# A two-layer graph network on one core: the late constants get due times of their own, and the one-hots are laid out block by block

## The chip, the core and the metric

The kernel runs on one core of a Trainium2 chip. A core has a matrix engine (TensorE, PE in the profile, with its weight loads as PEld), a vector engine (VectorE, DVE), an engine for copies and activation functions (ScalarE, ACT), a general engine (GpSimd, POOL) and a queue engine for transfers (SyncE, SP). Each runs its own list of instructions in order; semaphores join the lists. The metric is the time of one execution on the device in microseconds; several executions are run and their median is taken.

## The reference

Both layers work on 128 graphs of 128 nodes with 64 features, and a weighted adjacency matrix `adj` for each graph, of which about 6% of the entries are set.

```python
def _L0_gnn_ref(x, adj, W1, b1, W2, b2):
    mask = (adj > 0.0).astype(x.dtype)
    W1a, W1b = (W1[:F], W1[F:])
    xj_proj = x @ W1a
    diff = x[:, :, None, :] - x[:, None, :, :]
    h = jax.nn.relu(xj_proj[:, :, None, :] + diff @ W1b + b1)
    hm = jnp.einsum('bjkh,bjk->bjh', h, mask)
    deg = jnp.sum(mask, axis=-1)
    return hm @ W2 + deg[..., None] * b2
def _L1_gnn_ref(feat, adj, W1, b1, W2, b2, W3, b3):
    agg = jnp.einsum('bmn,bnd->bmd', adj, feat)
    h = jax.nn.elu(agg @ W1 + b1)
    h = jax.nn.elu(h @ W2 + b2)
    out = h @ W3 + b3
    return out
x = _layernorm(x + _L0_gnn_ref(...))
x = _layernorm(x + _L1_gnn_ref(...))
```

The costly part is layer 0: for each edge (j, k) a vector of 192 values, its relu, and the sum over the edges of each node j.

## The kernel before

**Pairs, blocks and units.** Two graphs make a pair; there are 64 pairs. The nodes of a graph are sorted by degree (`prepare`, `sort_x`, `sort_mask`), so that the sorted nodes fall into nine fixed blocks: nodes p0 to p1 of block i get s edge slots each, which makes n = s (p1 - p0) columns, between 66 and 170, and E = 1323 columns over all blocks. One block of one pair is a unit. A unit has three steps (`unit`): ScalarE copies the node's own part `aj` into one of four PSUM banks `e` (L910), TensorE adds the neighbours' part `cp` by 18 matmuls of a block's one-hot `oh` (L920, in three bf16 parts, three thirds of the 192 values, two graphs), and VectorE sums the absolute values over the slots into `sums` (L930). Bank u mod 4 is free for unit u + 4 when unit u is reduced. The one-hots say which neighbour each slot of each node takes; VectorE makes one block of both graphs by one comparison of the running count `vp` with the slot number `slotc` (L675).

**Around the units.** Each pair goes through `prepare` (mask `mk` L545, keys, ranks `cmp` L568, permutation `permb` L575), `sort_x` (sorted features, projection L606, `aj` L613, correction `ea` L635 with matmuls L626 and L629, `sa` L620, `corr` L642 on GpSimd), `sort_mask` (matmuls L246 and L248, `mtp`, `permT`, `vp` L668, then the nine one-hots), `turn` and `project_c` (`cp` through matmuls L708 and L711, casts L718, the rest `r` L722 on VectorE, L725, L727 on GpSimd). `finish` does the remainder: `hm` (L842), the projection L847 and L851, back to the old order L864, the norm (`y` L737, `st` L742), and layer 1 with L871, L880, L886, L893 and `h` (L797).

**What sets the order.** The program emits the instructions itself, in the order that `Flow` picks. Each piece of work is a thread, a generator whose steps name an engine, an estimated cost and what they come after. Every step has a due time in a model of the machine, taken from the table `DUE` and from the start of its pair, at 11.1651 units of the model per pair. Of the steps that the model says can start, `Flow.run` takes the one with the least due time; early on it first takes those that the model can start earliest. When a thread's list of due times has run out, all its later steps keep the last one. The chosen order is the order of every engine's list; on the chip only semaphores hold an instruction. These semaphores are put in from the tiles that instructions write and read.

**The late constants.** `consts_late` (L484 on) prepares what layer 1 and the second projection need: w2d (VectorE), v1p (ScalarE), a tile of ones (`onesf`), two matmuls for sums of weights (L504, L505), the biases `cc` (L508 to L510), the centred last weights (L512 to L519), and the last bias as three bf16 rows `rowp` (L521 and L362 to L366). They are 22 steps, nearly all on VectorE, each small and most waiting for the one before. The thread starts at half a pair before pair 0, with one due time for all its steps.

Of the kernel before, what the change touches and what calls it, by code (L numbers as in the profile page):

```python
# [32 lines left out]
BF16 = mybir.dt.bfloat16  # L33
# [153 lines left out]
def sparse(tc, env):  # L187

    g = type("env", (), dict(env))
    nc, P, N, F, H, O, HB, H1, NP, E = (  # L190
        g.nc, g.P, g.N, g.F, g.H, g.O, g.HB, g.H1, g.NP, g.E)
    LAY, NB = g.LAY, g.NB
    loads, prep, work, ps_m = g.loads, g.prep, g.work, g.ps_m
# [3 lines left out]
    flow = Flow([ps_m.tile([P, 512], F32, name=f"m{i}") for i in range(4)])  # L197
# [4 lines left out]
    ROUND = 11.1651  # L202
    AHEAD = 4

    DUE = {
        "prepare": (-43.06, -42.93, -39.21, -39.08, -35.87),
        "sort_x": (-26.76, -10.46, -10.33, -3.14, -3.02, 2.5, 2.63, 2.76, 2.89),
        "sort_mask": (-26.12, -25.99, -25.86, -23.42, -23.29, -23.16, -13.67, -13.28, -13.03,
                      -12.77, -2.63, -2.25, -1.99, -1.73),
        "turn": (-36.9, -36.77),  # L210
        "project_c": (-32.15, -29.32, -29.2, -29.07, -28.94, -4.17, -4.04),
        "finish": (12.64, 19.44, 19.57, 21.62, 21.75, 21.88, 22.01, 28.04, 28.17, 29.2, 33.56,
                   33.69, 33.82, 34.71, 43.31, 43.44, 44.47, 44.6, 46.52, 46.65, 48.06, 48.19,
# [2 lines left out]
                 (4.68, 4.81, 4.94), (5.07, 5.2, 5.33), (5.97, 6.1, 6.22), (6.35, 6.48, 6.61),  # L216
                 (7.25, 11.61, 11.74)],
    }

    def begin_thread(name, p, gen):  # L220
        flow.start(ROUND * p, DUE[name], gen)
# [262 lines left out]
    def consts_late():  # L484

        v = nc.vector

        def w2diag():
            for s in range(2):
                h = slice(s * HB, (s + 1) * HB)  # L490
                v.tensor_scalar(w2d[h, :, s, :], w2s[h], 0.5, None, op0=OP.mult)
        yield from op("DVE", 0.5, w2diag, "w2d", "w2", "w2d0")

        def v1diag():
            for s in range(2):
                nc.scalar.copy(v1p[s * F:(s + 1) * F, s, :], v1d[s * F:(s + 1) * F])
        yield from op("ACT", 0.6, v1diag, "v1p", "v", "v1p01")


        onesf = temp([P, P], F32, "onesf")  # L500
        yield from op("DVE", 0.2, lambda: v.memset(onesf, 1.0), "onesf")

        def sums(t):
            nc.tensor.matmul(t[:, O:O + 1], v2s, onesf[:, 0:1], start=True, stop=True)  # L504
            nc.tensor.matmul(t[:, :O], onesf, v3s, start=True, stop=True)  # L505
        ev, t = yield ("PE", 0.6, made("onesf", "v", "c"), 1, sums)
        c3 = rows[:, :O]
        ev, = yield ("DVE", 0.2, [ev], 0, lambda: v.tensor_sub(cc[:, 3:4], cc[:, 3:4], t[:, O:O + 1]))  # L508
        ev, = yield ("DVE", 0.2, [ev], 0, lambda: v.tensor_scalar(cc[:, 0:2], cc[:, 2:4], -1.0, None, op0=OP.mult))
        ev, = yield ("DVE", 0.2, [ev], 0, lambda: v.tensor_scalar(cc[:, 2:4], cc[:, 2:4], 1.0, None, op0=OP.add))  # L510
        happened(ev, "const", "cc")
        ev, = yield ("DVE", 0.2, [ev], 0, lambda: v.tensor_sub(c3, c3, t[:, :O]))  # L512
        flow.give(t, ev)

        for k, w in enumerate((v3s, c3)):
            m = mean[:, k:k + 1]
            for fn in (lambda: v.tensor_reduce(m, w, AX.X, OP.add),
                       lambda: v.tensor_scalar(m, m, 1.0 / O, None, op0=OP.mult),
                       lambda: v.tensor_scalar(w, w, m, None, op0=OP.subtract)):  # L519
                ev, = yield ("DVE", 0.2, [ev], 0, fn)  # L520
        ev, = yield ("DVE", 0.2, [ev], 0, lambda: v.tensor_copy(rows[:, O:], c3))  # L521
        happened(ev, "const", "v3s")
        happened(ev, "const", "rows")
        last = ["rows", "rowp0", "b2p"]
        for name, fn in parts(rows, rowp, NR):
            yield from op("DVE", 0.4, lambda: fn(nc.vector), "row" + name, *last)
            last = ["row" + name]
        happened(event("const", "row2"), "const", "rowp")
# [116 lines left out]
    def sort_mask(p, ev):  # L645

        d, a, permb = S[p], ADJ[p], S[p]["permb"]

        def sort(t):
            for s in range(2):  # L650
                stationary(t[:, s * N:(s + 1) * N], lambda h: d["mk"][:, s, h], permb[:, s, :],
                           start=True, stop=True)
            for s in range(2):
                stationary(t[:, (2 + s) * N:(3 + s) * N], lambda h: permb[:, s, h], identb,
                           start=True, stop=True)
        ev, t = yield ("PE:*", 0.22, [ev], 1, sort)
        mtp = d["mtp"] = prep.tile([P, 2, N], BF16, name="mtp", bufs=7)
        permT = d["permT"] = prep.tile([P, 2, N], F32, name="permT", bufs=7)
        evm, = yield ("ACT", act(2 * N), [ev], 0, lambda: nc.scalar.copy(flat(mtp), t[:, :2 * N]))
        happened(evm, "mtp", p)  # L660
        ev, = yield ("ACT", act(2 * N), [ev], 0, lambda: nc.scalar.copy(flat(permT), t[:, 2 * N:]))
        flow.give(t, ev)
        happened(ev, "permT", p)
        ev, vps = yield ("PE:*", 0.12, [evm] + made("prefix"), 1,
                         lambda vps: stationary(vps[:, :2 * N], lambda h: prefix[:, h], flat(mtp),
                                                start=True, stop=True))
        vp = prep.tile([P, 2, N], BF16, name="vp")
        ev, = yield ("ACT", act(2 * N), [ev], 0, lambda: nc.scalar.copy(flat(vp), vps[:, :2 * N]))  # L668
        flow.give(vps, ev)
        oh = d["oh"] = prep.tile([P, 2, E], BF16, name="oh", bufs=5)  # L670
        for i, (base, n, p0, p1, sl) in enumerate(LAY):
            w = p1 - p0
            c = slice(base, base + n)
            ev, = yield ("DVE PORT", 0.08 + n / 960, [ev] + made("slotc"), 0,
                         lambda: nc.vector.tensor_tensor(  # L675
                             oh[:, :, c].rearrange("p b (s w) -> p b s w", w=w),
                             vp[:, :, p0:p1].rearrange("p b (o w) -> p b o w", o=1)
                             .to_broadcast([P, 2, sl, w]),
                             slotc[:, c].rearrange("p (b s w) -> p b s w", b=1, w=w)
                             .to_broadcast([P, 2, sl, w]),  # L680
                             op=OP.is_equal))
            happened(ev, "oh", p, i)
# [219 lines left out]
    def unit(u, ev):  # L902
        p, i = units[u]
        d = S[p]
        base, n, p0, p1, sl = LAY[i]
        w = p1 - p0
        e = edges[u % NE][:, :3 * n]
        ev, = yield ("ACT", 0.09 + 3 * n / 1200,
                     [ev, event("aj", p)] + made("banks"), 0,
                     lambda: nc.scalar.copy(  # L910
                         e.rearrange("p (c s w) -> p c s w", c=3, w=w),
                         d["aj"][:, :, p0:p1].rearrange("p c (o w) -> p c o w", o=1)
                         .to_broadcast([P, 3, sl, w])))

        def gather():
            cp, oh = d["cp"], d["oh"]
            for k in range(3):
                for c in range(3):
                    for s in range(2):
                        nc.tensor.matmul(e[s * HB:(s + 1) * HB, c * n:(c + 1) * n],  # L920
                                         cp[:, k, s, c * HB:(c + 1) * HB],
                                         oh[:, s, base:base + n],
                                         start=False, stop=(k == 2), skip_group_check=True)
        flow.under_way = u < len(units) - 14
        ev, = yield ("PE:t", 0.03 + 0.0037 * n, [ev, event("cp", p), event("oh", p, i)], 0, gather)

        def reduce():
            if "sums" not in d:
                d["sums"] = work.tile([P, 3, N], F32, name="sums")
            nc.vector.tensor_reduce(d["sums"][:, :, p0:p1],  # L930
                                    e.rearrange("p (c s w) -> p c w s", c=3, w=w),
                                    AX.X, OP.add, apply_absolute_value=True)
        ev, = yield ("DVE", 0.07 + 3 * n / 960, [ev], 0, reduce)
        happened(ev, "sums", p, i)
        return ev
# [33 lines left out]
    flow.start(-97.0, [0.0], consts_wad())  # L969
    flow.start(DUE["sort_x"][2], [0.0], consts_b2())  # L970
    flow.start(-95.0, [0.0], consts_banks())
    flow.start(ROUND * -0.5, [0.0], consts_late())
    for k in range(NE):
        begin_unit(k, [0.0])
    arrive_late()
# [203 lines left out]
```

## Time and profile before

| what | value |
|---|---|
| runs | 758.67, 760.54, 761.2 us; median 760.54 us |
| the profiled execution | a span of 758.2 us from the first to the last instruction; the fastest run shown is 758.67 |
| mean granted clock of TensorE | 0.988 |
| gather matmuls L920 | 10368, 393.3 us busy |
| reduces L930 | 576, 334.4 us busy |
| copies into e, L910 | 576, 293.6 us busy |
| one-hots L675 | 576, 148.9 us busy |

The page gives each engine's busy time, slices of the span, the chain of work that ended last, and groups of instructions by line. In a line of the timeline the first number is the start, the second the length, then engine, source line, operation, what is written and read, and how many instructions were merged; in brackets stands how long the engine had been idle and who released it. A line of the waits names who waited for whom, the total, the number of times and the longest. Spans of one engine's neighbours overlap a little[...]. Windows give, for each engine, the busy time and the number of instructions in a stretch, then the granted clock of TensorE as a share of the full one, and the DMA share and rate.

### The profile page before, as it was taken

Reading aid. Unit: us, or ns where it says so; the run is one execution under the profiler, and the core shown is the slowest. Engines: PE = TensorE matmul, PEld = TensorE weight load, DVE = VectorE, ACT = ScalarE, POOL = GpSimd, SP = SyncE. Lnnn points to the kernel's source line nnn. Section 1 sums busy time; section 2 is a strip of 40 time slices with the busy share of each in tenths; the row PEclk is TensorE's granted clock in tenths of the full one; section 3 lists DMA queues with packets and bytes.
Section 4 is the critical chain, followed back from the end, with each engine's and each line's share of the span. In section 5 each row is a group of like instructions: output and inputs, shape, how many; then the busy total and the mean of one; then the engine's idle time right before and its main releaser. Section 6 shows DMA issues by size and latency. Waiting matters only on the chain.

```text
span 758.2 us, 36118 instructions
## 1 busy us (share of the span) xinstructions
PE 736.3 (97%) x14788; PEld 672.4 (89%) x14789; DVE 722.5 (95%) x2381; ACT 705.7 (93%) x1986; POOL 432.4 (57%) x801
## 2 busy tenths in 40 slices
PE   7699999999999999999999999999999999999994
PEld 4588999999999999999999999999999999999993
DVE  7799999999999999999999999999999999999984
ACT  4499999999999999999999999999999999999984
POOL 5255566566556557556556656655655655655662
PEclk9799999999999999999999999999999999999998
DMA  4000011011011011011101101101101101100000
GB/s 121 15 3 3 17 31 31 17 31 32 16 31 32 20 27 31 20 27 31 28 20 31 31 17 32 31 16 31 31 20 28 31 21 27 31 21 16 10 13 19
DMA packets 54667, 19.72 MB, mean 26 GB/s; under 512 B 37600, under 2 KB 54496, under 8 KB 54496
## 3 DMA queue, kind: packets, MB, share of 16 engines
q1 hardware_dynamic: 53792, 17.05, 9.3%
q8 instruction: 118, 1.93, 1.1%
q14 instruction: 53, 0.43, 0.2%
q10 hardware_dynamic: 704, 0.30, 0.2%
HBM read 13.14 MB, written 4.19 MB: 23 GB/s over the span
## 4 chain that ended last, share of the span: by engine, by line
PE 95%; DVE 2%; ACT 1%; DMA 1%; issue 0%; POOL 0%; POOLq 0%; SPq 0%; DVEq 0%; ACTq 0%
PE e L920 46%; PE m L606 6%; PE m L708 5%; PE m L847 5%; PE m L886 4%; PE m L880 4%; PE m L893 4%; PE m L864 3%; PE m L246 3%; PE m L690 3%; PE m L592 2%; PE m L871 2%; PE m L851 1%; PE m L711 1%; PE m L248 1%; PE m L691 1%
## 5 line engine op out<-in xcount | busy, mean ns | idle before, releaser
L920 PE MATMUL e<-oh,cp 128*64 128x162 bf16 (+3 forms) x10368 | 393.3, 229 | 6.0 <-DVE oh L675 5.6
L920 PEld LDWEIGHTS <-cp 128*64 128x64 bf16 x10368 | 357.8, 110 | 18.3 <-issue 6.6
L930 DVE TENSOR_REDUCE sums<-e 128x54 f32<-128x486 f32 (+8 forms) x576 | 334.4, 608 | 10.2 <-PE e L920 4.6
L910 ACT COPY e<-aj 128x504 f32<-128x504 f32 (+6 forms) x576 | 293.6, 543 | 3.1 <-DVE sums L930 2.6
L749 POOL TENSOR_SCALAR ve<-st 128x2 f32<-128x2 f32 x126 | 24.1, 191 | 242.4 <-DVE st L742 237.0
L675 DVE TENSOR_TENSOR oh<-vp,slotc 128x308 bf16<-128x308 bf16 (+6 forms) x576 | 148.9, 315 | 4.8 <-ACT vp L668 1.3
L750 POOL TENSOR_TENSOR rs<-ve,mhalf 128x2 f32<-128x2 f32 x126 | 87.8, 697 | 10.5
L727 POOL TENSOR_TENSOR cp<-r,cp 128x512 bf16<-128x512 f32 x64 | 74.5, 1164 | 32.0 <-ACT cp L725 32.0
L642 POOL TENSOR_TENSOR corr<-ea,sa 128x384 f32<-128x384 f32 x64 | 64.3, 1005 | 16.5 <-DVE ea L635 11.5
L791 ACT ACTIVATE r<-m,cc 128x256 f32<-128x256 f32 x128 | 61.4, 480 | 5.2 <-PE m L880 3.2
L842 POOL TENSOR_TENSOR hm<-sums,corr 128x384 f32<-128x384 f32 x63 | 63.2, 1004 | 4.0 <-DVE sums L930 4.0
L620 POOL TENSOR_TENSOR sa<-aj,srow 128x384 f32<-128x384 f32 x64 | 64.3, 1005 | 1.0 <-ACT aj L613 1.0
L613 ACT ACTIVATE aj<-m,b1c 128x128 f32<-128x128 f32 x192 | 56.5, 366 | 8.2 <-PE m L606 1.2
L797 DVE SCALAR_TENSOR_TENSOR h<-m,cc,e 128x256 f32<-128x256 f32 x128 | 60.3, 471 | 2.0 <-ACT e L794 1.9
L794 ACT ACTIVATE e<-r 128x256 f32<-128x256 f32 x128 | 54.4, 426 | 2.1
L606 PE MATMUL m<-xsT,wad 128*128 128x128 f32 x384 | 53.7, 276 | 0.0
L847 PE MATMUL m<-w2d,hm 128*128 128x128 f32 x384 | 53.5, 276 | 0.0
L722 DVE TENSOR_TENSOR r<-m,cp 128x256 f32<-128x256 f32 x128 | 47.7, 414 | 1.6 <-ACT cp L718 1.6
L771 ACT ACTIVATE x<-y,nb,rs 128x64 f32<-128x64 f32 x126 | 49.0, 441 | 0.2 <-POOL nb L753 0.2
L718 ACT CAST cp<-m 128x256 bf16<-128x256 f32 x128 | 40.3, 366 | 8.8 <-PE m L711 8.8
L847 PEld LDWEIGHTS m<-w2d,hm 128*128 128x128 f32 x384 | 48.0, 192 | 0.3 <-POOL hm L842 0.3
L606 PEld LDWEIGHTS m<-xsT,wad 128*128 128x128 f32 x384 | 47.9, 192 | 0.4
(157 smaller groups left out, 1350.3 us busy)
## 6 DMA issues: line engine op xcount, KB each, us to landing
adj<-in_adj_dram SPq DMA_DIRECT2D x64, 128.0 KB, 2.9
xx<-in_x_dram SPq DMA_DIRECT2D x64, 64.0 KB, 2.6
out_dram<-o SPq DMA_DIRECT2D x64, 64.0 KB, 1.6
w1s<-in_L_gnn_W_dram ACTq DMA_DIRECT2D x2, 96.0 KB, 3.2
w2s<-in_L_gnn_W_dram ACTq DMA_DIRECT2D x2, 48.0 KB, 3.0
v2s<-in_L_gnn_W_dram SPq DMA_DIRECT2D x1, 64.0 KB, 2.2
v1d<-in_L_gnn_W_dram SPq DMA_DIRECT2D x2, 32.0 KB, 2.1
rows<-in_L_gnn_b_dram SPq DMA_DIRECT2D x1, 64.0 KB, 5.6
```

The source lines that it names most:

```text
L606: nc.tensor.matmul(aps[:, c * N:(c + 1) * N], wad[:, c, :], xsT, start=True, stop=True)
L620: evs, = yield ("POOL PORT", 1.0, [have] + made("srow"), 0, lambda: nc.gpsimd.tensor_mul(sa, aj, srow))
L642: ev, = yield ("POOL PORT", 1.05, [ev, evs], 0, lambda: nc.gpsimd.tensor_sub(corr, ea, sa))
L675: lambda: nc.vector.tensor_tensor(oh[:, :, c].rearrange("p b (s w) -> p b s w", w=w), vp[:, :, p0:p1].rearrange("p b (o w) -> p b o w", o= ...
L727: lambda: nc.gpsimd.tensor_sub(cp[:, 2], r1, cp[:, 1]))
L750: nc.gpsimd.tensor_tensor(rs, ve, mhalf, op=OP.pow)
L791: lambda: nc.scalar.activation(r, z, AF.Relu, bias=c, scale=-1.0))
L842: lambda: (nc.vector if late else nc.gpsimd).tensor_sub(hm, d["sums"], d["corr"]))
L847: nc.tensor.matmul(yb[:, :2 * O], hm[:, c, :], flat(w2d[:, c]), start=(c == 0), stop=False)
L910: lambda: nc.scalar.copy(e.rearrange("p (c s w) -> p c s w", c=3, w=w), d["aj"][:, :, p0:p1].rearrange("p c (o w) -> p c o w", o=1) .to_br ...
L920: nc.tensor.matmul(e[s * HB:(s + 1) * HB, c * n:(c + 1) * n], cp[:, k, s, c * HB:(c + 1) * HB], oh[:, s, base:base + n], start=False, stop ...
L930: nc.vector.tensor_reduce(d["sums"][:, :, p0:p1], e.rearrange("p (c s w) -> p c w s", c=3, w=w), AX.X, OP.add, apply_absolute_value=True)
```

## The change

The late constants get a list of 22 due times, from 12.0 to 36.0, counted from the start of pair 0, in place of one due time for all. So every step has a due time of its own, among those of the first pairs.

The tile of the one-hots keeps its size. Before, it was one run of E columns for the first graph and one for the second, and block i lay at columns base to base + n of both. Now block i lies in columns 2 base to 2 (base + n), first the n columns of the first graph, then the n of the second. The comparison writes there, and the gather reads there.

```diff
+    DUE["consts_late"] = (
+        12.0, 17.0, 18.5, 19.5, 19.65, 19.66, 19.67, 19.68, 23.0, 24.0, 25.0, 26.0, 27.0, 28.0,
+        29.0, 30.0, 31.0, 32.0, 33.0, 34.0, 35.0, 36.0)
+
     def begin_thread(name, p, gen):
...
-        oh = d["oh"] = prep.tile([P, 2, E], BF16, name="oh", bufs=5)
+        oh = d["oh"] = prep.tile([P, 2 * E], BF16, name="oh", bufs=5)
         for i, (base, n, p0, p1, sl) in enumerate(LAY):
             w = p1 - p0
             c = slice(base, base + n)
             ev, = yield ("DVE PORT", 0.08 + n / 960, [ev] + made("slotc"), 0,
                          lambda: nc.vector.tensor_tensor(
-                             oh[:, :, c].rearrange("p b (s w) -> p b s w", w=w),
+                             oh[:, 2 * base:2 * (base + n)].rearrange("p (b s w) -> p b s w", b=2, w=w),
...
                         nc.tensor.matmul(e[s * HB:(s + 1) * HB, c * n:(c + 1) * n],
                                          cp[:, k, s, c * HB:(c + 1) * HB],
-                                         oh[:, s, base:base + n],
+                                         oh[:, 2 * base + s * n:2 * base + (s + 1) * n],
                                          start=False, stop=(k == 2), skip_group_check=True)
...
-    flow.start(ROUND * -0.5, [0.0], consts_late())
+    flow.start(0.0, DUE["consts_late"], consts_late())
```

## The prediction

> **What bounds the kernel now.** I read the page first: where the span goes, and who holds the chain.
>
> ```profile
> span 758.2 us, 36118 instructions
> PE 736.3 (97%) x14788; PEld 672.4 (89%) x14789; DVE 722.5 (95%) x2381; ACT 705.7 (93%) x1986; POOL 432.4 (57%) x801
> PE 95%; DVE 2%; ACT 1%; DMA 1%; issue 0%; POOL 0%; POOLq 0%; SPq 0%; DVEq 0%; ACTq 0%
> ```
>
> TensorE is the bound, VectorE 2 points behind. So only what leaves TensorE idle, or slow, is worth anything. Second view, the waits of TensorE over the whole span: its longest line is one single wait, in the start-up.
>
> ```profile
> PE e L920 <- DVE oh L675: 5.6, 1, 5.6
> ```
>
> Third, the timeline of TensorE; of it the starts of block 0's gather for pairs 0, 1, 2, 3 and 4:
>
> ```profile
> 21.88 0.26 PE L920 MATMUL e<-oh,cp 128*64 128x162 bf16 x1
> 27.70 1.37 PE L920 MATMUL e<-oh,cp 128*64 128x162 bf16 x17 [5.57 <-DVE oh L675]
> ...
> 39.30 0.83 PE L920 MATMUL e<-oh,cp 128*64 128x162 bf16 x18 [0.46 <-ACT e L910]
> ...
> 49.34 0.80 PE L920 MATMUL e<-oh,cp 128*64 128x162 bf16 x18
> ...
> 60.07 0.80 PE L920 MATMUL e<-oh,cp 128*64 128x162 bf16 x18
> ...
> 70.81 0.80 PE L920 MATMUL e<-oh,cp 128*64 128x162 bf16 x18
> ```
>
> The reader is to see that the first gather's first matmul runs at 21.88 and its second waits for VectorE. Pair by pair the distance is 11.60, 10.04, 10.73, 10.74 us, then (82.05 - 70.81) 11.24 for the rest. Fourth, VectorE at that place:
>
> ```profile
> 15.45 0.34 DVE L675 TENSOR_TENSOR oh<-vp,slotc 128x324 bf16<-128x324 bf16 x1
> ...
> 20.35 0.15 DVE L508 TENSOR_TENSOR cc<-cc,m 128x1 f32<-128x1 f32 x1 [0.54 <-ACT e L910]
> ...
> 26.03 0.18 DVE L366 COPY rowp<-low 1x128 bf16<-1x128 bf16 x1
> 26.23 1.92 DVE L675 TENSOR_TENSOR oh<-vp,slotc 128x132 bf16<-128x132 bf16 x8
> 29.11 0.66 DVE L930 TENSOR_REDUCE sums<-e 128x54 f32<-128x486 f32 x1 [0.97 <-PE e L920]
> ```
>
> Block 0's one-hot of pair 0 was written at 15.45, yet TensorE waits until pieces of the run that starts at 26.23. Those are other blocks and pair 1. A block's two batch halves lie E columns apart, so the stretch from a block's first to its last element covers nearly all other blocks; a dependence kept by such a stretch joins blocks that share nothing. Between 20.35 and 26.21 VectorE does the late constants, each step waiting for the one before (0.68 us for cc and rows, then 3.2 from 23.03 on, with pair 2's r between). Last, busy time and granted clock in windows of 1 us, and of one later pair:
>
> ```profile
> 22.00:23.00 1.00, 0.13 (x1) 0.00 (x0) 0.64 (x2) 1.00 (x5) 0.00 (x0) 1.00 0.00 0
> 24.00:25.00 1.00, 0.00 (x0) 0.00 (x0) 0.86 (x5) 0.00 (x0) 0.00 (x0) 0.50 0.00 0
> 33.00:34.00 1.00, 1.00 (x22) 1.00 (x19) 0.84 (x3) 0.59 (x1) 0.17 (x1) 0.50 0.00 0
> 35.00:36.00 1.00, 1.00 (x35) 1.00 (x32) 0.97 (x3) 0.95 (x2) 0.46 (x1) 1.00 0.06 16
> 84.67:95.91 11.24, 11.24 (x237) 10.35 (x235) 11.06 (x37) 10.97 (x33) 6.66 (x13) 1.00 0.11 26
> ```
>
> The clock (third column from the right) halves during the stall and is full again only from about 34. A later pair has TensorE busy for all of its 11.24 us.
>
> **What the Trainium skill says.** "TensorE: Matmul & The Clock Gate", Part 1 (The HAM clock gate): a window of some 3.4 us of idleness halves the clock, sustained work restores it. The trace agrees on the fall (idle from 22.1, half from 24) and is slower on the return (work from 27.7, full at 34). "Vector Engine (DVE) Microarchitecture Reference", section 5.1: an operation on two 16-bit tensors makes two results a cycle when all step by one; pairs may span rows, and 4-byte alignment makes no difference. The trace agrees: one-hots of 336 elements follow each other by 0.245 us, of 132 by 0.152, which is 0.46 ns an element. No page bears on how the dependences are kept.
>
> **The change, part by part.** The two compiled instruction lists, laid side by side, show what moves.
>
> *Layout.* No instruction is added or removed. In the changed list the second matmul of the first gather carries no VectorE wait any more, nor does pair 1's; two waits of one-hots on earlier one-hots go too. The stall of 5.57 us goes. The matmuls still read n adjacent columns, and their pitch of 70 ns for 162 columns already is the streaming rate, so nothing is gained per gather. For the one-hots I take 0 per instruction; bounds are 15 ns less (the two blocks of 308 elements differ by that, 0.226 and 0.240) and 15 ns more. Either is hidden from pair 4 on: VectorE's groups of that period, each mean less the 0.08 us by which the next one overlaps it, come to 10.9 us of 11.24 (9 reduces 4.75, 9 one-hots 2.1, h 0.8, r 0.65, cmp 0.55, ea 0.5, mk 0.4, bn 0.4, permb 0.35, y 0.4).
>
> *Due times.* The w2d and v1p steps stay ahead of the first gather (v1p 0.63 us of ScalarE, moved behind five copies, with ScalarE idle for 1.68 us in this stretch). Of the rest the onesf memset stays too, 18 VectorE steps and the two matmuls of the sums leave the head. DMA issues keep their order on SP. The list puts them so: sums matmuls, cc and rows, and the first mean in pair 1; eleven steps in pair 2; two in pair 3. In return pair 2's projection, pair 3's mask sort (before at 36.19) and pair 4's keys come ahead of the first gather on TensorE, and on GpSimd pair 1's cp (1.2) ahead of sa, which nobody needs before corr.
>
> **The sum, along VectorE.** I follow VectorE, since with the stall gone it has more to do per early pair than TensorE. Start to start of block 0's reduce it needs, before, 8.3 us in pair 0, 9.8 in pairs 1 and 2, 10.55 in pair 3 (the terms above without the finish steps not yet there); TensorE's own work there is 7.9, 9.4, 10.15, 10.7.
>
> 1. First gather. ScalarE's aj and e copies follow pair 0's projection as before: projection at about 18.9 (it now waits for pair 3's permb, 18.35), aj 19.8 to 20.7, e copy to 21.6. Gather at 21.7, as before within 0.2, but all of it: done 22.45, reduce at 22.7 (before 29.11).
> 2. Pair 0: VectorE 8.3 plus the compare of pair 4, 0.55, that moved in, plus 1.2 of waits: it outruns gathers 1 and 2, which stand behind pair 3's projection (0.7), and ea waits for its matmuls, which wait for r. Pair 1's first reduce: 22.7 + 10.05 = 32.75.
> 3. Pair 1: 9.8, plus the cc string 0.7 (20.35 to 21.03 above), plus a mean 0.1, plus 0.9 of a new wait: cc needs the sums matmuls, which stand on TensorE behind pair 0's L847 and L851. Behind cc on VectorE stand nine one-hots, y and the last reduce; all are late by it. 32.75 + 11.5 = 44.25.
> 4. Pair 2: 9.8 plus eleven constant steps at their durations less the same overlap, 1.55: 55.6.
> 5. Pair 3: 10.55, two copies 0.2, 0.1 lost: 66.45.
>
> Before, pair 4's first reduce followed its gather (70.81) by 0.88, at 71.69. Gain 5.2. From pair 4 on VectorE has 0.3 us a pair in hand and TensorE is the bound again; its gathers then may stand up to 0.4 nearer to the reduces (the smallest distance from an e copy's end to its gather in a later pair is 0.37). So 5.6 us. The half-clock stretch, some 3.2 us of TensorE (6.35 busy at 0.5), and the stall are both gone, 8.8 together; 3.2 of it is given back to VectorE. What is late next is VectorE's constants in pairs 1 and 2. The order of everything after pair 3 is unchanged, and so is the tail.
>
> Profiled execution: 758.2 - 5.6 = 752.6 of span. The runs shown are 758.67 to 761.2 with median 760.54, so the profiled execution was near the fastest; the same 5.6 off the median gives 754.9.
>
> **Rivals.**
> *TensorE alone decides.* VectorE's small steps cost less than their records and its waits vanish in the slack: stall 5.57, clock 3.2 and the 0.46 before 39.30 come back, 9.2 us: 751.3. For it: the e banks let four gathers run ahead. Against: the VectorE sums above exceed TensorE's in each of pairs 0 to 2.
> *The stall moves.* cc's wait in pair 1 or new gaps ahead of the first gather grow to 2 or 3 us, or the clock falls again because TensorE pauses around 25: 2.5 us remain, 758.0. For it: TensorE is 74% busy between 15 and 20, and keeps full clock there; little more is in hand.
> *It doesn't do what it says.* The gather meets another late release at 27 (cp, e, a bank): 760.5. Against: ScalarE stood idle 1.68 us and then 6.55 behind TensorE, GpSimd from 20.6.
> *Slower: the one-hots lose their pace.* With the output as one run of 2n they drop to one result a cycle. Section 5.2 of that page gives 1.04 ns an element at one per cycle, so twice the rate saves 0.52; an estimate from it, for 294 elements on average, is 0.153 us more, nine a pair: 1.38, against 0.3 in hand, 1.1 x 63 pairs = 69 us: about 824. It decides from 35 ns per one-hot. Against: dtype and steps are as before, and the inputs already run in rows of w.
>
> **How the numbers follow.** Forecast 0.63; TensorE alone 0.12; stall moves 0.13; nothing 0.07; one-hots slower 0.05. A difference of 0.3%, 2.3 us, is about what a measurement of this kernel can tell from none. Forecast and TensorE alone are faster by more, and of "stall moves" most: 0.86. Same 0.09, slower 0.05. The forecast's own range, with 15 ns either way per early one-hot (0.4 over three pairs), 1 us for the waits of steps 2 and 3 and the runs' spread of 1.2, is 752.5 to 757; to leave out no more than two in ten it runs from 751 to 758.
>
> **What would show it.** Right: no TensorE wait on oh; first gather in one piece near 21.7; full clock from 20 on; reduces back to back in pairs 1 and 2; a short VectorE wait before cc near 40; pair 4's first gather near 65. Wrong: a half clock after 25, one-hot means above 0.36, a period other than 11.24 after pair 5, or a first gather well off 21.7.

## The result and the profile after

| | before | after |
|---|---|---|
| median of five runs | 759.63 us | 753.9 us |
| lowest to highest | 758.67 to 761.2 | 752.54 to 754.12 |
| span of the profiled execution | 758.2 us | 752.3 us |
| mean granted clock of TensorE | 0.988 | 0.992 |
| gather matmuls, busy | 393.3 us | 385.5 us |
| pair 4's first gather starts | 70.81 us | 68.21 us |
| one later pair | 11.24 us | 11.18 us |

The ratio of the runs after to the runs before is 0.9921, with a 95% interval of 0.9907 to 0.9934. The page of the kernel after, its head and its first group:

```profile
span 752.3 us, 36121 instructions
PE 732.1 (97%) x14791; PEld 667.8 (89%) x14792; DVE 724.3 (96%) x2381; ACT 706.3 (94%) x1986; POOL 432.1 (57%) x801
...
L924 PE MATMUL e<-oh,cp 128*64 128x162 bf16 (+3 forms) x10368 | 385.5, 228 | 3.5 <-ACT e L914 3.3
```

TensorE is still the bound. The same 10368 matmuls take 7.8 us less (in part since none of them runs at half clock any more, as the windows below show), and none of their idle time is put down to the one-hots any more. The waits of TensorE after, the longest lines of those that concern the first pairs (total, times, longest):

```profile
PE e L924 <- ACT e L914: 3.3, 7, 1.0
...
PE m L712 <- DVE r L726: 1.7, 2, 1.2
...
PE m L630 <- DVE r L726: 1.2, 1, 1.2
```

The wait of 5.6 us on the one-hots is gone; none of these is longer than 1.2 us. The timeline of TensorE after gives block 0's gathers of pairs 0, 1, 4 and 5:

```profile
22.46 0.82 PE L924 MATMUL e<-oh,cp 128*64 128x162 bf16 x18 [0.32 <-ACT e L914]
...
32.27 0.82 PE L924 MATMUL e<-oh,cp 128*64 128x162 bf16 x18 [0.46 <-ACT e L914]
...
68.21 0.80 PE L924 MATMUL e<-oh,cp 128*64 128x162 bf16 x18
...
79.39 0.80 PE L924 MATMUL e<-oh,cp 128*64 128x162 bf16 x18
```

The first gather runs in one piece, 18 matmuls. But pair 4 starts only 2.60 us earlier than before (70.81 - 68.21), less than half of the gain in time. From there each pair takes 11.18 us in place of 11.24. The windows of the kernel after, columns as in those of before:

```profile
18.00:19.00 1.00, 1.00 (x9) 0.35 (x6) 1.00 (x5) 0.52 (x2) 0.47 (x1) 0.50 0.61 156
...
25.00:26.00 1.00, 0.58 (x22) 0.48 (x19) 0.75 (x2) 0.76 (x3) 0.00 (x0) 1.00 0.00 0
33.00:34.00 1.00, 1.00 (x20) 0.60 (x18) 1.00 (x3) 0.64 (x2) 0.10 (x1) 1.00 0.00 0
68.21:79.39 11.18, 11.18 (x235) 10.29 (x233) 11.13 (x38) 10.66 (x30) 6.66 (x12) 1.00 0.01 4
```

Two things are to be seen. TensorE is busy for the whole of a later pair, as before, and the pair is shorter all the same: so the matmuls themselves became faster. And the half clock between 24 and 34 is gone, but in this execution another half-clock stretch stands at 18, ahead of the first gather. Two of the five runs, with a mean clock of 0.995, took 752.54 and 752.71 us; the other three, with 0.992 or 0.993, took 753.9 to 754.12.

So the gain of 5.9 us of span is about 2.6 in the start-up and 3.3 in the pairs after it, where the difference grows by 0.06 us a pair.

### The profile page after: what moved, and what is told of

Read it like the earlier page. It is cut to its first block, busy times and chain, and to the rows that moved or that the text cites. A ratio compares the mean times of both kernels' runs of the same rounds, so it can differ in the third digit from the quotient of the medians.

```text
span 752.3 us, 36121 instructions
## 1 busy us (share of the span) xinstructions
PE 732.1 (97%) x14791; PEld 667.8 (89%) x14792; DVE 724.3 (96%) x2381; ACT 706.3 (94%) x1986; POOL 432.1 (57%) x801
## 4 chain that ended last, share of the span: by engine, by line
PE 93%; DVE 3%; ACT 2%; issue 1%; DMA 0%; POOL 0%; ACTq 0%; POOLq 0%; DVEq 0%
PE e L924 45%; PE m L610 6%; PE m L851 5%; PE m L712 5%; PE m L890 4%; PE m L884 4%; PE m L897 4%; PE m L868 3%; PE m L694 3%; PE m L250 3%; PE m L596 2%; PE m L875 2%; PE m L855 1%; PE m L715 1%; PE m L252 1%; PE m L695 1%
## 5 line engine op out<-in xcount | busy, mean ns | idle before, releaser
L924 PE MATMUL e<-oh,cp 128*64 128x162 bf16 (+3 forms) x10368 | 385.5, 228 | 3.5 <-ACT e L914 3.3
L924 PEld LDWEIGHTS <-cp 128*64 128x64 bf16 x10368 | 350.2, 110 | 16.6 <-issue 4.9
L934 DVE TENSOR_REDUCE sums<-e 128x54 f32<-128x486 f32 (+8 forms) x576 | 335.1, 611 | 6.8 <-PE e L924 2.0
L679 DVE TENSOR_TENSOR oh<-vp,slotc 128x308 bf16<-128x308 bf16 (+6 forms) x576 | 150.3, 321 | 1.0 <-ACT vp L672 0.2
L851 PE MATMUL m<-w2d,hm 128*128 128x128 f32 x384 | 53.7, 276 | 0.0
L775 ACT ACTIVATE x<-y,nb,rs 128x64 f32<-128x64 f32 x126 | 49.1, 442 | 0.2 <-POOL nb L757 0.2
L851 PEld LDWEIGHTS m<-w2d,hm 128*128 128x128 f32 x384 | 48.0, 192 | 0.4 <-POOL hm L846 0.4
L712 PE MATMUL m<-wc,turned 64*128 64x256 f32 x256 | 46.4, 436 | 1.7 <-DVE r L726 1.7
```

The source lines that it names most:

```text
L679: lambda: nc.vector.tensor_tensor(oh[:, 2 * base:2 * (base + n)].rearrange("p (b s w) -> p b s w", b=2, w=w), vp[:, :, p0:p1].rearrange("p ...
L712: nc.tensor.matmul(cps[s][:, :cols], d["turned"][k, 2, :], wc[k, :], start=True, stop=False)
L851: nc.tensor.matmul(yb[:, :2 * O], hm[:, c, :], flat(w2d[:, c]), start=(c == 0), stop=False)
L934: nc.vector.tensor_reduce(d["sums"][:, :, p0:p1], e.rearrange("p (c s w) -> p c w s", c=3, w=w), AX.X, OP.add, apply_absolute_value=True)
```

## The experiments

Each kernel was run four or five times (`due_only` 21 times) beside runs of the kernel before; ratios are to the kernel before, with 95% intervals. Within a gather the matmuls come two by two, one for each graph of the pair, and the two run side by side. "Pitch" is the distance from the start of one graph's matmul to the start of the same graph's next one, in nanoseconds: the mean over a gather, and of that the median over the 64 pairs.

### Which half of the diff brings the gain

**The layout alone** (`layout_only`), the kernel after with the constants where they were:

```diff
-    flow.start(0.0, DUE["consts_late"], consts_late())
+    flow.start(ROUND * -0.5, [0.0], consts_late())
```

> The changed layout with the late constants back at the start. Theory VectorE head: the first gather no longer waits, but VectorE gets to the first reduce only at about 28.2, after the constants; from there 8.3, 9.8, 10.7 and 10.7 us to pair 4's first reduce at about 68 (the changed kernel 69.2, before 71.7); with the period of 11.18 some 7 us in all, 753 us, ratio 0.991, so no worse than the changed kernel. Rival: the due times carry the head's gain; then pair 4 starts near 70.5 and the ratio is 0.995 or more.

Measured: 753.99 us, ratio 0.9924 [0.991, 0.9937], with the period at 11.18. The layout alone gives all that the whole change gives. Its timeline of TensorE shows the wait in another place:

```profile
21.27 0.82 PE L924 MATMUL e<-oh,cp 128*64 128x162 bf16 x18
...
28.82 4.35 PE L924 MATMUL e<-oh,cp 128*64 128x168 bf16 x72 [2.33 <-ACT e L914]
```

The first gather no longer waits, but VectorE is at the constants and reduces nothing until 27.45, so the four banks fill up, ScalarE's copy comes late and TensorE waits 2.33 us. Pair 4's gather starts at 67.44 all the same.

**The due times alone** (`due_only`), the kernel before with the list of due times and the new start of the thread:

> The late constants at their own due times, the layout as before. Theory VectorE head: the first gather waits for the last one-hot written ahead of it, about 23.5 in place of 27.7, no half clock after it; then the same long stretches of VectorE as the changed kernel, so 1 to 2 us better than before in the head and a period of 11.24: about 758 us, ratio 0.998. Rival: the due times carry the head's gain of the prediction, 5.6 us: 754.5, ratio 0.9925.

Measured: 759.02 us, ratio 0.9992 [0.9985, 0.9999]. By themselves the due times are worth at most 0.15%. TensorE's waits on the one-hots are still there, three of them, 2.5 us in all, the longest 1.2, and pair 4's gather starts at 70.02, only 0.8 us earlier than before.

### Why a later pair is shorter

In the tile of before, the second graph's half lies E = 1323 columns behind the first, an odd number: in every block exactly one of the two halves starts at an odd column of a bf16 tile. After, both start at even columns in all blocks but block 6, whose n is 169. Two runs test the start columns alone.

**`align_only`**: the kernel before, with the tile one column wider for each graph and each block starting at an even column; the wait on the one-hots stays.

```diff
-        oh = d["oh"] = prep.tile([P, 2, E], BF16, name="oh", bufs=5)
+        oh = d["oh"] = prep.tile([P, 2, E + E % 2], BF16, name="oh", bufs=5)
...
-                                         oh[:, s, base:base + n],
+                                         oh[:, s, base + base % 2:base + base % 2 + n],
```

> The kernel before, with each half of a one-hot block starting at an even bf16 column (one column more per graph, blocks 7 and 8 shifted by one); blocks of a graph still lie apart, constants where they were. Theory start address: the gather's matmuls stream faster from an even start, so the pair's period falls from 11.24 to about 11.18 us, some 3.6 us over 60 pairs, ratio 0.995, while the 5.6 us wait at 22 stays. Rival dependences: the shorter period comes from waits that went with the layout; then the period stays 11.24 and the ratio is 1.000.

Measured: 755.88 us, ratio 0.9954 [0.994, 0.9967]. The wait of 5.6 us is still in the list of waits, and the pairs are short (timeline of TensorE, pairs 4 and 5):

```profile
69.57 0.80 PE L920 MATMUL e<-oh,cp 128*64 128x162 bf16 x18
...
80.75 0.80 PE L920 MATMUL e<-oh,cp 128*64 128x162 bf16 x18
```

**`odd_start`**: the kernel after, with everything moved by one column, so that 17 of the 18 halves start at an odd one.

```diff
-        oh = d["oh"] = prep.tile([P, 2 * E], BF16, name="oh", bufs=5)
+        oh = d["oh"] = prep.tile([P, 2 * E + 1], BF16, name="oh", bufs=5)
...
-                                         oh[:, 2 * base + s * n:2 * base + (s + 1) * n],
+                                         oh[:, 2 * base + 1 + s * n:2 * base + 1 + (s + 1) * n],
```

> The changed kernel with its one-hots shifted by one column, so that all halves but one start at an odd bf16 column. Theory start address: the period goes back to 11.24 us or beyond, and of the gain only the head's 2.6 us is left, about 757 us, ratio 0.9965. Rival dependences: these are as in the changed kernel, so the period stays 11.18 and the time is the changed kernel's, ratio 0.992.

Measured: 756.58 us, ratio 0.9965 [0.9951, 0.9978], and the long pairs are back (pairs 4 and 5):

```profile
66.65 0.80 PE L924 MATMUL e<-oh,cp 128*64 128x162 bf16 x18
...
77.89 0.80 PE L924 MATMUL e<-oh,cp 128*64 128x162 bf16 x18
```

The pitches of the nine blocks, for the matmuls of the first and of the second graph of a pair; a star marks a half that starts at an odd column:

| block (n) | 0 (162) | 1 (66) | 2 (168) | 3 (112) | 4 (168) | 5 (154) | 6 (169) | 7 (154) | 8 (170) |
|---|---|---|---|---|---|---|---|---|---|
| before, first | 70.5 | 34.4 | 72.6 | 49.5 | 73.2 | 66.9 | 73.4 | 69.6* | 76.8* |
| before, second | 70.4* | 34.9* | 73.4* | 50.2* | 73.6* | 69.6* | 73.9* | 66.9 | 76.8 |
| after, first | 70.0 | 34.6 | 72.5 | 49.1 | 72.5 | 66.6 | 73.4 | 66.8 | 76.4 |
| after, second | 70.0 | 34.6 | 72.5 | 49.1 | 72.5 | 66.6 | 73.9* | 66.8 | 76.4 |
| odd_start, first | 70.9* | 34.8* | 73.4* | 50.0* | 73.4* | 67.5* | 73.9* | 68.4* | 77.2* |
| odd_start, second | 70.9* | 35.6* | 73.4* | 50.0* | 73.4* | 67.5* | 73.4 | 68.5* | 77.2* |

`align_only`, where all halves start even, lies within 0.4 ns of the kernel after, and has 73.4 for the second graph in block 6 too. From before to after the nine differences come to 5.0 ns for the first graph's matmuls and 7.3 for the second's; a gather has nine such distances, so 0.045 to 0.066 us a pair, against 0.06 measured. What decides is whether the matmul's moving operand (the one-hot that is streamed through the array) starts at an odd or an even column: `align_only` and `odd_start` change that and nothing else. Blocks 5 and 7 show it inside one trace: both have 154 columns, in the kernel before the second half is odd in one and the first in the other, and the odd half is the slow one both times. Block 6 shows it between the kernel after and `odd_start`.

The two graphs' matmuls so drift apart. In the kernel before the second graph's starts on average 2 ns behind the first's in block 0 and 44 ns behind in block 6; in blocks 7 and 8, where the first graph's half is the odd one, that falls to 36 and 2. In the kernel after it is 3 to 7 ns throughout.

The Trainium skill ("TensorE: Matmul & The Clock Gate", Back-to-back issue gap) states n / 2.4 + 2.5 ns for a matmul by itself at the full clock, 66.7 for 154 columns. The even starts of blocks 0, 2 to 5 and 7 are within 0.2 ns of it, and 69.6 is above it; blocks 1 (34.6 against 30.0), 6 (73.4 against 72.9) and 8 (76.4 against 73.3) are above it at even starts too. Why 154 columns lose 2.8 to 3.0 ns where one half is odd, and only 0.9 to 1.7 where both are, is open.

### Why the start-up gained only 2.6 us

Two terms of VectorE were suspected: a wait for the sums matmuls in pair 1, and constant steps that take much longer in their new place. The timeline of VectorE after shows both:

```profile
41.01 0.16 DVE L512 TENSOR_TENSOR cc<-cc,m 128x1 f32<-128x1 f32 x1 [1.05 <-ACT ys L859]
...
46.56 0.74 DVE L523 TENSOR_SCALAR v3s<-v3s,mean 128x64 f32<-128x64 f32 x1
...
51.20 0.58 DVE L523 TENSOR_SCALAR rows<-rows,mean 128x64 f32<-128x64 f32 x1
...
58.26 1.04 DVE L370 COPY rowp<-mid 1x128 bf16<-1x128 bf16 x1
```

The last three took 0.25, 0.25 and 0.18 us in the kernel before, so they take 1.68 us more in all. Their lines in VectorE's timeline of before:

```profile
23.46 0.25 DVE L519 TENSOR_SCALAR v3s<-v3s,mean 128x64 f32<-128x64 f32 x1
...
24.07 0.25 DVE L519 TENSOR_SCALAR rows<-rows,mean 128x64 f32<-128x64 f32 x1
...
25.83 0.18 DVE L366 COPY rowp<-mid 1x128 bf16<-1x128 bf16 x1
```

There GpSimd ran nothing from 20.64 to 32.18. The timeline of GpSimd after, at the places of the three long steps:

```profile
46.25 1.00 POOL L846 TENSOR_TENSOR hm<-sums,corr 128x384 f32<-128x384 f32 x1
...
50.56 1.16 POOL L731 TENSOR_TENSOR cp<-r,cp 128x512 bf16<-128x512 f32 x1 [1.00 <-ACT cp L729]
...
58.24 1.00 POOL L846 TENSOR_TENSOR hm<-sums,corr 128x384 f32<-128x384 f32 x1
```

Each of the three starts while a GpSimd tensor operation runs and ends within 0.06 us of that operation's end (47.30, 51.78 and 59.30 against 47.25, 51.72 and 59.24).

**`port_free`**: the first reading was that these steps block because they have one source, and that forms with two sources would not. The steps became operations on two SBUF tensors.

```diff
...
-                       lambda: v.tensor_scalar(w, w, m, None, op0=OP.subtract)):
+                       lambda: v.tensor_tensor(w, w, m.to_broadcast([P, O]), op=OP.subtract)):
...
-        ev, = yield ("DVE", 0.2, [ev], 0, lambda: v.tensor_copy(rows[:, O:], c3))
+        ev, = yield ("DVE", 0.2, [ev], 0, lambda: v.tensor_tensor(rows[:, O:], c3, c3, op=OP.max))
...
-            yield from op("DVE", 0.4, lambda: fn(nc.vector), "row" + name, *last)
+            yield from op("DVE", 0.4, lambda: fn(Two), "row" + name, *last)
```

`Two` writes each copy of the bf16 rows, the copy of mid among them, as the maximum of a tile with itself.

> The changed kernel; its constants' VectorE steps with one tensor operand (subtracting the mean from v3s and from rows, and the copies and casts of rows) are written as operations with two tensor operands (the mean as a broadcast, a copy as the maximum of a tile with itself). Theory shared port: the three steps that took 0.74, 0.58 and 1.04 us ended with GpSimd's running operation; with two tensor operands they take at most 0.3 us, pair 4's first gather comes some 1.5 us earlier than 68.2, and the ratio to before is 0.990. Rival: the long steps waited for their operands; then they stay as long, and the ratio stays 0.992.

Measured: 753.2 us, ratio 0.992 [0.9906, 0.9935]. The steps stayed long (0.77, 0.60 and 1.03 us) and again ended with GpSimd's operation, within 0.08 us. So this reading fell. The Trainium skill ("SBUF — State Buffer", SBUF: two separate sides) says why it had to, if the page holds here: the port pair that VectorE shares with GpSimd is taken both by VectorE's two-port fast modes and by operations with two SBUF inputs (these only against a GpSimd operation that reads SBUF), and whoever comes second waits for the whole instruction. The rewrite had put one kind in place of the other.

The one-hots, which have two SBUF inputs, give a second look at that. In the kernel after, only 8 of the 576 share time with a GpSimd operation, because the program's model keeps them apart. Two that start well inside one are these: one of 132 elements took 1.21 us from 18.69 to 19.90 (its kind takes 0.24), another, of 336 elements, took 1.12 from 21.98 to 23.10 (its kind takes 0.33). They end 0.11 and 0.20 us after the GpSimd operation. The records of L679 between 18.6 and 18.8 (least, median and longest in ns), and then GpSimd's timeline:

```profile
L679 DVE TENSOR_TENSOR oh<-vp,slotc x2: 323/766/1208, 18.5 to 18.7; 128x336 bf16<-128x336 bf16 x1, 128x132 bf16<-128x132 bf16 x1
```

```profile
18.52 1.27 POOL L731 TENSOR_TENSOR cp<-r,cp 128x512 bf16<-128x512 f32 x1 [0.78 <-ACT cp L729]
21.75 1.15 POOL L624 TENSOR_TENSOR sa<-aj,srow 128x384 f32<-128x384 f32 x1 [1.96 <-ACT aj L617]
```

VectorE operations with a source in PSUM run beside GpSimd at their usual length: L741 takes 0.29 us beside it (62 records) and 0.28 otherwise (66), the reduce L934 of 462 elements to 33 sums 0.633 beside it (57 records) and 0.632 otherwise (7). But so does one kind whose only source lies in SBUF: of the 128 operations `mk<-adj`, 114 start while a GpSimd tensor operation runs, and none takes more than 0.29 us. Their line in the groups of VectorE (busy us, mean ns of one, idle time before):

```profile
L549 DVE TENSOR_SCALAR_CACHE_REDUCE mk<-adj 128x128 bf16<-128x128 f32 x128 | 31.0, 281 | 1.3 <-DMA adj<-in_adj_dram 1.3
```

So more than a semaphore can hold up a step on the chip; but that all sources lie in SBUF is not what makes a VectorE operation wait, though the theory of the next run says so.

**`port_kept`** planned the constant steps like the one-hots, as users of the shared port:

```diff
-                ev, = yield ("DVE", 0.2, [ev], 0, fn)
+                ev, = yield ("DVE PORT", 0.2, [ev], 0, fn)
```

> The changed kernel; the eleven VectorE steps of the late constants from the first mean to the bf16 rows are planned like the one-hots, which the program's model never lets run beside a GpSimd tensor operation; nothing is computed differently. Shared-port theory (a VectorE operation whose sources all lie in SBUF and that starts beside a GpSimd tensor operation ends only after it): the three long steps (0.74, 0.58, 1.04 us) fall to 0.3 or less wherever they no longer start beside one, pair 4's first gather moves from 68.21 to about 66.7, ratio to before about 0.990. Rival (these steps wait for their own operands or semaphores): they stay long in their new places although GpSimd is idle there, gather and ratio stay at 68.2 and 0.992.

Measured: 753.03 us, ratio 0.992 [0.9906, 0.9933]. The due times decided the order as before, the steps stayed beside the same GpSimd operations, and took 0.74, 0.57 and 1.04 us. This run tells nothing of the cause.

**`port_apart`** moved them where GpSimd pauses:

```diff
-        12.0, 17.0, 18.5, 19.5, 19.65, 19.66, 19.67, 19.68, 23.0, 24.0, 25.0, 26.0, 27.0, 28.0,
-        29.0, 30.0, 31.0, 32.0, 33.0, 34.0, 35.0, 36.0)
+        12.0, 17.0, 18.5, 19.5, 19.65, 19.66, 19.67, 19.68, 19.69, 19.7, 19.71, 26.0, 27.0, 28.95,
+        29.0, 30.0, 31.0, 32.0, 33.0, 34.0, 34.01, 34.02)
```

> The changed kernel; seven due times moved so that the three long VectorE steps fall where GpSimd pauses: the v3s step just after cc, the rows step behind the next reduce, the mid copy just behind the hi copy. Same operations, same counts. Shared-port theory: with GpSimd idle they take 0.25, 0.25 and 0.18 us as before the change, VectorE has 1.6 us less to do in pairs 1 to 3, and pair 4's first gather moves from 68.21 to about 66.6, ratio about 0.990. Rival (the length belongs to the steps' own operands): 0.74, 0.58 and 1.04 stay, gather at 68.2, ratio 0.992.

Measured: 751.87 us, ratio 0.9904 [0.989, 0.9918]. The timeline of VectorE:

```profile
42.24 0.24 DVE L523 TENSOR_SCALAR v3s<-v3s,mean 128x64 f32<-128x64 f32 x1
...
52.05 0.26 DVE L523 TENSOR_SCALAR rows<-rows,mean 128x64 f32<-128x64 f32 x1
...
56.21 0.18 DVE L370 COPY rowp<-mid 1x128 bf16<-1x128 bf16 x1
```

And of GpSimd, where the brackets give its pauses ahead of these operations:

```profile
45.25 0.19 POOL L753 TENSOR_SCALAR ve<-st 128x2 f32<-128x2 f32 x1 [5.92 <-DVE st L746]
...
56.22 0.23 POOL L753 TENSOR_SCALAR ve<-st 128x2 f32<-128x2 f32 x1 [4.51 <-DVE st L746]
```

The first two steps lie in these pauses, and the third starts 0.01 us ahead of the end of the second. The same operations have their old length where GpSimd pauses, and pair 4's gather starts at 66.98, 1.23 us earlier (1.6 were expected). The length belonged to the place, not to the operations. That the shared port is what holds them is the skill's account; the runs show that they end with GpSimd's operation, and that they don't lengthen away from it.

**`sums_early`**: the tile of ones and the two matmuls of the sums get due times 11 and 12, before pair 0's L851, so that cc needn't wait.

```diff
-        12.0, 17.0, 18.5, 19.5, 19.65, 19.66, 19.67, 19.68, 23.0, 24.0, 25.0, 26.0, 27.0, 28.0,
+        12.0, 17.0, 11.0, 12.0, 19.65, 19.66, 19.67, 19.68, 23.0, 24.0, 25.0, 26.0, 27.0, 28.0,
```

> The changed kernel with the tile of ones and the two sums matmuls due at 11 and 12 in place of 18.5 and 19.5, so that they stand on TensorE ahead of pair 0's second projection. Theory: the 1.05 us that VectorE idles ahead of cc at 41.0 goes, and since VectorE sets the pace there until pair 4, the kernel gains about 1 us: ratio 0.991. Rival: the idle time is made up for by slack in pairs 2 and 3; ratio 0.992 as in the changed kernel.

Measured: 751.11 us, ratio 0.9891 [0.9876, 0.9907]. The idle 1.05 us ahead of cc is gone, and from pair 1's first reduce to pair 2's VectorE takes 10.44 us in place of 11.58. From the first gather to pair 4's it takes 44.60 us in place of 45.75. The profiled execution also had the full clock ahead of the first gather, which started at 20.83 in place of 22.46; part of the gain over the kernel after is that.

### Versions that take VectorE's constants away

**`consts_pool`**: `sums_early`, with the steps after cc and the row sums on GpSimd.

```diff
...
-                       lambda: v.tensor_scalar(m, m, 1.0 / O, None, op0=OP.mult),
-                       lambda: v.tensor_scalar(w, w, m, None, op0=OP.subtract)):
...
+                           ("POOL", lambda: q.tensor_scalar(m, m, 1.0 / O, None, op0=OP.mult)),
+                           ("POOL", lambda: q.tensor_tensor(w, w, m.to_broadcast([P, O]), op=OP.subtract))):
...
-            yield from op("DVE", 0.4, lambda: fn(nc.vector), "row" + name, *last)
+            yield from op("POOL", 0.3, lambda: fn(nc.gpsimd), "row" + name, *last)
```

> The changed kernel with the sums matmuls early, and all constant steps after cc and the two row sums on GpSimd in place of VectorE, at the same due times. Theory: VectorE's extra work in pairs 1 to 3 sets the start-up, so pair 4's first gather comes about 4 us earlier than 68.2 (1.7 us of port waits, 1.0 of idle time, 1.5 of work), about 750 us, ratio 0.987. Rival: TensorE or GpSimd takes over as the bound of the start-up, gain under 2 us, ratio 0.990 or more.

Measured: 749.49 us, ratio 0.9867 [0.985, 0.9885]; pair 4's gather starts at 64.47. From the first gather to pair 4's it takes 42.11 us, against 44.60 in `sums_early` and 45.75 in the kernel after. TensorE's work is the same in the three: so it was VectorE's work that set the pace there.

**`consts_pool_head`**: the new layout, these steps on GpSimd, and the thread at its old place before pair 0.

> The new layout with the late constants at the start as before, but their steps after cc and the two row sums on GpSimd. Theory: VectorE reaches the first reduce about 3 us earlier than with the constants in its own list (27.4), and no constants come later, so pair 4's first gather stands near 64.5 and the time is about 751 us, ratio 0.988. Rival: the constants' chain on GpSimd holds up pair 0's corr and pair 1's cp, and the ratio is 0.991 or more.

Measured: 749.52 us, ratio 0.9877 [0.986, 0.9895]. The intervals of the two overlap: once the steps are off VectorE, the due times make no difference that can be seen here either.

**`consts_pool_even`**: `consts_pool` with block 6's second half one column further, so that all 18 halves start at even columns.

> The kernel with the sums early and the constants on GpSimd, and in addition block 6's second half moved by one column, so that all 18 halves start at an even bf16 column. Start-address theory: block 6's pitch falls from 73.9 to about 73.0 ns per pair of matmuls, 0.008 us a pair of graphs, 0.5 us in all: 749.0, ratio about 0.986; the period goes from 11.18 to 11.17. If the odd start of one half costs nothing by itself: pitch 73.9 and 749.5 stay.

Measured: 748.48 us, ratio 0.9866 [0.9851, 0.9881]. The second graph's pitch in block 6 went from 73.9 to 73.4, half of what was expected, and the period from 11.181 to 11.176. The ratio can't tell it from `consts_pool`. It has the lowest median of all, and the three versions of this section are clearly ahead of the kernel after (0.9921).

## Why the prediction came out, and where it was wrong

The time was within its range, 1.0 us from the forecast. Two of its terms were wrong by about 3 us each, with opposite signs, so that the total came out is luck as far as these two go.

**The stall went, as forecast.** No wait on the one-hots is left, the first gather is in one piece, and the clock is full from 21 on. That it was the distance between the two halves that joined the blocks is borne out by two runs: in `align_only` they still lie apart and the wait of 5.6 us stays, in `layout_only` they lie together and it is gone with the constants at their old place. That VectorE would then set the start-up is borne out by `consts_pool`. Cc's wait was forecast at 0.9 near 40 and is 1.05 at 41.01.

**The head term was mis-sized: 5.6 forecast, 2.60 measured.** The steps of the sum, by block 0's reduces:

| step | forecast us | measured us | difference |
|---|---|---|---|
| 1, first reduce at | 22.7 | 23.39 | +0.69 |
| 2, pair 0 | 10.05 | 10.27 | +0.22 |
| 3, pair 1 | 11.5 | 11.58 | +0.08 |
| 4, pair 2 | 11.35 | 11.97 | +0.62 |
| 5, pair 3 | 10.85 | 12.0 | +1.15 |

These sum to 2.76; the remaining quarter of a microsecond is the 0.4 that pair 4's gather was to gain on its reduce, of which 0.13 came (it starts 1.01 us ahead of the reduce, before 0.88).

- Steps 1 and 2 go with the clock. The projection at 19.16 took 1.60 us at half clock (0.50 in the windows from 18 to 20), and aj, the e copy and the gather came late behind it. `odd_start` has the same order, and its profiled execution kept the full clock there:

```profile
18.00:19.00 1.00, 0.62 (x6) 0.43 (x4) 1.00 (x2) 1.00 (x5) 1.00 (x1) 1.00 0.44 112
```

In it the projection takes 0.89 us, the first gather starts at 20.81, the first reduce at 22.52, and pair 0 takes 9.51; `sums_early`, with the full clock and even starts, has 22.52 and 9.51 too. Part of that lead is older: two matmuls of L252 take 0.42 us at 11.44 in the kernel after and 0.28 at 11.38 in `odd_start`, so the full clock first came later in the kernel after, and at 17.49 it is 0.68 us behind. With the clock of `odd_start` the forecast of steps 1 and 2 together is 0.7 us too long (32.75 against 32.04), and pair 4's gather stands at 66.65 there, 4.2 us earlier than before. The text had the danger among its rivals, for a pause near 25; it came at 17.
- Steps 4 and 5: the constants were charged "at their durations", which were those of a place where GpSimd was idle. In the new place the v3s and rows steps take 0.49 and 0.33 more, which more than covers step 4, and the copy of mid 0.86 more, which is most of step 5. In `port_apart`, without that, pair 3 takes 10.62.

**"Nothing is gained per gather" was wrong.** The pitch of 70 ns for 162 columns was taken for the rate of all blocks. Block 0 happens to be one of those that hardly pay for an odd start; that the two graphs' matmuls of block 5 run at 66.9 and 69.6 for the same 154 columns was in the trace of before, and shows that something other than the count of columns matters. The text asked after alignment for VectorE's write alone, where nothing is to be seen, and not for TensorE's read. About 60 pairs at 0.06 us are 3.3 us of the result, and the mark "a period other than 11.24 after pair 5" was hit.

**The fall of the clock was read too kindly.** The text has the trace agree with a window of some 3.4 us of idleness. In the kernel before the clock fell 1.7 us into the stall (22.13 to 23.87), and in the kernel after at 17.2, where no pause of TensorE was longer than 1.16 us.

**The sum didn't price the two halves of the diff apart, and the due times are worth nothing that these runs can tell.** They were to clear VectorE's way to the first reduce, which they do (23.39, against 27.45 in `layout_only`), and to give 3.2 us back later. With cc's wait and the stretched steps all of it is given back: pair 4 starts at 68.21 with them (66.65 in `odd_start`, with the full clock) and at 67.44 without.

**The rivals.** "TensorE alone decides" and "it doesn't do what it says" are out by the gathers. "The stall moves" was right in kind for cc and for a falling clock, but too small to leave 758.0. "The one-hots lose their pace": their busy time is 150.3 us against 148.9, and the two long ones beside GpSimd alone have 1.8 too much; per instruction the layout costs nothing to be seen.

## What to carry to other kernels

When a layout change moves where an operand starts, compare the pitch for operands of the same size and other starts before calling a rate the rate: here the starts alone gave 0.5%. Price a moved step by what the neighbour engines do at its new place, since a short VectorE step beside a one-microsecond GpSimd operation can cost all of it (not every kind does: find out which). And a total that comes out right proves no term of its sum; compare it with the profile stage by stage.

## What the hardware showed unexpectedly

- A bf16 moving operand of a matmul that starts at an odd column streams slower: where one graph's half was odd, by 0.3 to 3.0 ns a matmul (154 columns 69.6 against 66.6, 112 columns 50.2 against 49.1). That both halves are odd costs no more in sum than one: the period was 11.24 us in both cases.
- Two matmuls that run side by side keep a pace of their own: the slower one fell behind by up to 44 ns over seven gathers, and caught up when the other became the slower.
- VectorE steps of 0.18 to 0.25 us took up to 1.04 beside a GpSimd tensor operation and ended with it, within 0.06 us; one-hots of 0.24 and 0.33 took 1.21 and 1.12 and ended 0.1 and 0.2 us after it. `mk<-adj`, with its source in SBUF, kept its 0.28 us beside one.
- TensorE's clock halved for 3.4 us ahead of the first gather, after 3.4 us in which TensorE was busy for 1.97 and paused for 1.16 at most. The profiled execution of `odd_start` has the same pause and 2.01 us busy in that stretch, and kept the full clock. What decides is open.
